# Linear attention's output projection: x seeded into the PSUM banks by identity matmuls and copied back by ScalarE

## The chip, the cores and the metric

The kernel runs on one core of one Trainium2 chip. The metric is the device time of that core in microseconds, from one execution of the whole program; the comparison uses the median of several executions. Five engines of the core appear below: TensorE (PE, with its weight loads listed apart as PEld), VectorE (DVE), ScalarE (ACT), GpSimd (POOL) and SyncE (SP), which only issues transfers here.

## The reference, cut to what matters

The program is a chain of eight residual blocks on `x` of shape (4, 512, 256): four sequences of 512 tokens with 256 channels. Each block adds its result to `x`, or rather to the `x` that the block before it left. The change lies in the fifth block, a gated linear attention with 16 heads; the sixth block, a "workspace" feed-forward, reads the `x` that it leaves.

```python
x = x + _L1_attn_a_ref(_layernorm(x), Wq, Wk, Wv, Wg, Wgk1, Wgk2, bgk2, norm_w, Wo)
x = x + _L1_ffn_ref(_layernorm(x), ...)

def _L1_attn_a_ref(x, ...):            # b = 4, t = 512, h = 16, dk = 8, dv = 16
    q = (x @ Wq).reshape(b, t, h, dk) * scale
    k = (x @ Wk).reshape(b, t, h, dk)
    v = (x @ Wv).reshape(b, t, h, dv)
    gk = jax.nn.log_sigmoid(x @ Wgk1 @ Wgk2 + bgk2) / 16
    def step(S, inp):
        qt, kt, vt, gt = inp
        S = S * jnp.exp(gt)[..., None] + kt[..., None] * vt[..., None, :]
        return S, jnp.einsum('bhk,bhkv->bhv', qt, S)
    _, o = jax.lax.scan(step, S0, (qT, kT, vT, gT))
    g = (x @ Wg).reshape(b, t, h, dv)
    o = o * rsqrt(mean(o * o, -1) + EPS) * norm_w
    o = o * (g * sigmoid(g))
    return o.reshape(b, t, vd) @ Wo     # the projection that the change touches
```

All data are float32.

## The kernel before

**Tiles.** `x[b]` is an SBUF tile of 128 partitions by 4 blocks by 256 channels, one for each sequence, and stays there for the whole program. PSUM has eight banks of 128 x 512 float32. In the linear attention stage they are handed out by three tags: `st` (two buffers of two banks, method `st()`), `two` (one buffer of two banks, method `two()`) and `acc` (two buffers of one bank, method `ps()`). Because `two` has a single buffer, whoever asks for it next waits until the one before has been read out.

**The stage** is `gla_stage` and its inner function `run`. It goes through the four sequences in order, with four steps each (`m` = 0 to 3). The names that the prediction uses:

- `states(b, n, pair)`: TensorE spreads the values into an `st` buffer (L877), VectorE multiplies it by the keys (L878), and two VectorE scans run along the 512 tokens (L881). GpSimd multiplies the scanned states by the queries (L886). Two calls in each step.
- `reads(b, n, qs)`: TensorE sums over the key channels into `acc` banks (L896). It runs one step late. On odd steps ScalarE squares the result (L904) and copies it out (L908), and GpSimd multiplies it by the gate (L910).
- `gate(b)`: at step 0, TensorE projects the gate into `two` (L231, the tile pair `ps_two<-own_xt,s`), and ScalarE applies Silu (L864).
- `output(b, 0)`: TensorE sums the squares over a head (L231, `ps_acc<-gsq,s4b`), VectorE and ScalarE form the reciprocal root (L919 to L926). `output(b, 1)` spreads it with an identity matmul (L231, `ps_acc<-grs,ident`) and VectorE multiplies the result by it (L935; for the last sequence L930 does that directly).
- `output(b, 2)` calls `project_add`, which multiplies by the weights `wo` and adds to `x[b]`. For the first three sequences it uses `two`: eight matmuls of 256 columns (L231, `ps_two<-s,go`), then one VectorE addition over 128 x 1024 (L990). For the last sequence (`halves`) it uses two `acc` banks and two VectorE additions (L988).

**The order of the work.** TensorE's instructions run in the order in which the program writes them (`manual_schedule`). A planner, which simulates the program when it is built, sets the order on the other engines by its own estimates; each engine then runs its list strictly in that order. The program order around the change is this:

```python
if m == 0:
    gate(b)
    if k > 1:
        output(order[k - 2], 2)      # the projection of two sequences ago
...
reads(*held)
output(order[-1], 0)
output(order[-2], 2)                 # the third sequence's projection
self.keep(8, self.st()[:, 0, :])     # eight matmuls with unused results
output(order[-1], 2)                 # the last sequence's, in halves
```

So the first and second sequence's projection stand behind the gate of the third and the fourth sequence; the third's stands in the tail of the stage, ahead of eight filler matmuls (L237) and the last projection.

**What follows `x[b]`.** The next block, method `ws`, takes the layer norm of each `x[b]`: VectorE statistics (L178, L179), a reciprocal root (L141 to L147 on GpSimd for the first two sequences, L154 to L160 otherwise) and ScalarE's normalisation into `ws_xf` (L196), then TensorE transposes (L1096) with copies by ScalarE (L1099) and VectorE (L1100). The planner puts the statistics of the first three sequences into the linear attention stage, directly behind the addition to that `x[b]`.

Of the kernel before, what the change touches and what calls it, by code (L numbers as in the profile page):

```python
# [13 lines left out]
ALU = mybir.AluOpType  # L14
AX = mybir.AxisListType

P = 128
# [4 lines left out]
NC = D // P  # L22
# [3 lines left out]
class Model:  # L26
# [949 lines left out]
    def project_add(self, b, ot, wo, halves=False):  # L976

        if halves:
            pys = [self.ps().rearrange("p (i d) -> p i d", d=D) for _ in range(2)]
        else:  # L980
            py = self.two().rearrange("p a (i d) -> p (a i) d", d=D)
            pys = [py[:, :2], py[:, 2:]]
        for i in range(NI):
            self.mm(pys[i // 2][:, i % 2, :], [(ot[:, c, i * P : (i + 1) * P], wo[:, c, :]) for c in range(NC)])
        x = self.x[b]
        if halves:
            for k, p in enumerate(pys):
                self.nc.vector.tensor_tensor(x[:, 2 * k : 2 * k + 2], x[:, 2 * k : 2 * k + 2], p, op=ALU.add)  # L988
        else:
            self.nc.vector.tensor_tensor(x, x, py, op=ALU.add)  # L990

# [825 lines left out]
```

## Time and profile before

| What | Value |
|---|---|
| Median of 3 runs | 2170.89 us (2170.74 to 2171.37) |
| The profiled execution's own time | 2171.51 us |
| Its span, first to last instruction | 2169.5 us |
| Mean granted TensorE clock | 0.965 of full |
| TensorE matmul busy | 2002.6 us (92%) |
| VectorE busy | 1270.7 us (59%) |
| ScalarE busy | 761.9 us (35%) |
| GpSimd busy | 576.6 us (27%) |

The profile comes from one execution. A row of a group gives the line of the kernel, the engine, the operation, the tile written and the tiles read, the shape and the count; behind the first bar stand the busy time in us and the mean ns of one instruction, behind the second the engine's idle time just before the group and who ended it. A float32 matmul of 128 x 512 appears as two records, so the counts of TensorE are twice the number of matmuls in the program. The chain is the path of work that ended last, in order of time, with start and duration in us.

The state matmuls of the linear attention stage (L877) start between 1401.7 us and 1569.0 us of the span; with the last projections the stage ends shortly before 1600 us. It is about a tenth of the span. VectorE's three additions of L990 start at 1501.8, 1546.3 and 1587.0 us.

### The profile page before, as it was taken

The page shows a single profiled execution, that of the slowest core. Times are in us where ns is not written, and L with a number is a line of the kernel's source. Part 1 is how long each engine was busy: PE and PEld are TensorE (multiplying, and loading weights), DVE is VectorE, ACT ScalarE, POOL GpSimd, SP SyncE. Part 2 cuts the span into 40 slices and gives each one's busy share as a digit, 9 for nine tenths or more (in the row PEclk, how much of TensorE's full clock was granted, in tenths as well). Part 3 has the DMA queues.
Part 4 walks back from the last instruction along what each step waited for, and adds up shares of the span by engine and source line. Part 5 has one row for each costly group of instructions (what it writes and reads, how often), then busy time and mean ns, then how long its engine had stood idle before and what let it go on. Part 6 is the DMA issues. An engine that isn't in the chain of part 4 may idle for free.

```text
span 2169.5 us, 25634 instructions
## 1 busy us (share of the span) xinstructions
PE 2002.6 (92%) x9418; PEld 1069.5 (49%) x9418; DVE 1270.7 (59%) x3180; ACT 761.9 (35%) x1700; POOL 576.6 (27%) x530
## 2 busy tenths in 40 slices
PE   7999999999899999999999999987888889989886
PEld 4556555564544554544454554533345644544464
DVE  5565655756546435644754355498854766666545
ACT  2433444434323222322232233244234334334542
POOL 2333332433312112221312122175620022222100
PEclk9999999999999999999999999989799999999898
DMA  4020000000000000000000000010000000000001
GB/s 176 1 90 1 1 1 1 1 1 1 21 0 0 1 0 0 0 1 0 0 1 0 1 0 1 18 28 0 1 25 1 1 1 1 1 1 2 1 1 40
DMA packets 19838, 22.87 MB, mean 11 GB/s; under 512 B 4833, under 2 KB 17665, under 8 KB 19329
## 3 DMA queue, kind: packets, MB, share of 16 engines
q1 hardware_dynamic: 19712, 21.24, 2.9%
q8 instruction: 74, 1.21, 0.2%
q14 instruction: 52, 0.42, 0.1%
HBM read 19.14 MB, written 2.10 MB: 10 GB/s over the span
## 4 chain that ended last, share of the span: by engine, by line
PE 63%; DVE 16%; issue 11%; ACT 5%; POOL 3%; DMA 1%; SPq 0%; POOLq 0%; DVEq 0%; ACTq 0%
PE ps_two L231 26%; PE ps_acc L231 11%; PE ps_two L383 5%; PE ps_acc L422 3%; PE ps_two L1493 3%; DVE ps_two L249 3%; PE ps_two L410 2%; POOL e L680 2%; PE ps_two L1536 2%; DVE gs L881 1%; PE ps_acc L1241 1%; DVE ln_st L178 1%; PE ps_two L647 1%; ACT prob L390 1%; PE ps_acc L638 1%
## 5 line engine op out<-in xcount | busy, mean ns | idle before, releaser
L680 POOL TENSOR_TENSOR e<-e 128x1024 f32<-128x1024 f32 x64 | 150.6, 2353 | 619.6 <-ACT e L672 592.4
L249 DVE CUSTOM_DVE_ANT_0 ps_two<-ps_two,mask 128x256 f32<-128x256 f32 (+3 forms) x512 | 249.8, 503 | 71.2 <-PE ps_two L383 41.5
L672 ACT ACTIVATE e<-ps_two 128x1024 f32<-128x1024 f32 x128 | 130.6, 1022 | 348.6 <-PE ps_two L231 348.4
L231 PE MATMUL ps_acc<-e,cv 128*128 128x512 f32 x512 | 235.0, 602 | 1.4 <-DVE cot L678 0.9
L231 PE MATMUL ps_two<-cq,ckt 128*128 128x512 f32 x512 | 232.2, 596 | 3.0 <-DVE cq L649 3.0
L395 POOL TENSOR_TENSOR prob<-prob,psum_row 128x256 f32<-128x256 f32 (+3 forms) x128 | 159.5, 1254 | 283.4 <-DVE psum_row L394 277.2
L390 ACT ACTIVATE prob<-ps_two,nmax 128x128 f32<-128x128 f32 (+3 forms) x256 | 132.3, 524 | 147.3 <-DVE nmax L249 138.1
L231 PEld LDWEIGHTS ps_acc<-e,cv 128*128 128x128 f32 x512 | 93.5, 190 | 138.3 <-issue 116.7
L231 PEld LDWEIGHTS ps_two<-cq,ckt 128*128 128x128 f32 x512 | 97.2, 191 | 118.1 <-issue 115.9
L231 PE MATMUL ps_two<-own_xt,s 128*128 128x512 f32 x200 | 110.8, 687 | 18.7 <-DVE prt L129 10.6
L231 PE MATMUL ps_two<-own_xt,s16a 128*128 128x512 f32 x256 | 114.9, 593 | 0.1
L231 PE MATMUL ps_two<-s16b,cot 128*128 128x256 f32 x512 | 113.1, 379 | 0.0
L383 PE MATMUL ps_two<-kvt,qx 64*128 64x256 f32 (+3 forms) x512 | 103.9, 483 | 6.3 <-ACT qx L371 2.4
L1525 ACT ACTIVATE lo_ex<-ps_two 128x1024 f32<-128x1024 f32 (+3 forms) x128 | 85.3, 704 | 69.5 <-PE ps_two L1493 65.9
L410 PEld LDWEIGHTS ps_two<-ident,prob 128*128 128x128 f32 x640 | 71.1, 142 | 73.7 <-issue 48.4
L231 PEld LDWEIGHTS ps_two<-s16b,cot 128*128 128x128 f32 x512 | 97.3, 190 | 20.0 <-issue 7.7
L410 PE MATMUL ps_two<-ident,prob 128*128 128x128 f32 x640 | 94.6, 279 | 12.7 <-ACT qx L371 4.5
L1526 POOL TENSOR_SCALAR_AFFINE_SELECT lo_ex<-lo_ex 128x256 f32<-128x256 f32 x128 | 51.5, 406 | 188.1 <-ACT lo_ex L1525 186.9
L681 DVE TENSOR_TENSOR es<-e 128x512 f32<-128x512 f32 x64 | 43.9, 686 | 94.9 <-POOL e L680 93.8
L383 PE MATMUL ps_two<-kpe,qy 64*128 64x256 f32 (+3 forms) x512 | 90.8, 432 | 0.9 <-POOL qy L317 0.9
L1493 PE MATMUL ps_two<-lo_qm,lo_t 32*128 32x128 f32 (+3 forms) x512 | 75.8, 473 | 11.1 <-ACT lo_ex L1525 4.7
L422 PE MATMUL ps_acc<-prt,kv 128*64 128x256 f32 (+3 forms) x512 | 77.2, 444 | 2.7 <-DVE prt L129 2.7
(428 smaller groups left out, 3423.3 us busy)
## 6 DMA issues: line engine op xcount, KB each, us to landing
x<-in_x SPq DMA_DIRECT2D x4, 512.0 KB, 7.4
s16b<-in_mla_wo SPq DMA_DIRECT2D x1, 2048.0 KB, 18.3
s16a<-in_cos_wq SPq DMA_DIRECT2D x1, 2048.0 KB, 9.9
s16b<-in_cos_wo SPq DMA_DIRECT2D x1, 2048.0 KB, 8.3
out_x<-x SPq DMA_DIRECT2D x4, 512.0 KB, 2.9
s16a<-in_mla_wqn SPq DMA_DIRECT2D x1, 1536.0 KB, 12.2
s<-in_mla_wqa SPq DMA_DIRECT2D x1, 1024.0 KB, 9.2
s4a<-in_mla_wkb SPq DMA_DIRECT2D x1, 512.0 KB, 6.6
```

The source lines that it names most:

```text
L231: self.nc.tensor.matmul(out, lhsT=l, rhs=r, start=k == 0, stop=k == n - 1)
L249: self.nc.vector.tensor_tensor_reduce(out=sc[:, :n], in0=sc[:, :n], in1=self.mask[:, T - n :], scale=-1.0, scalar=3.0e38, op0=ALU.add, op1 ...
L383: nc.tensor.matmul(sc[:, k, :n], lhsT=q[r, rows], rhs=key[r, :n], start=first, stop=not first)
L390: nc.scalar.activation(pr[:, k, :n], sc[:, k, :n], AF.Exp, bias=nm[:, k : k + 1], scale=-1.0, accum_out=sm[:, k : k + 1],)
L395: nc.gpsimd.tensor_tensor(pr[:, :, :n], pr[:, :, :n], sm.unsqueeze(2).to_broadcast([P, 2, n]), op=ALU.mult)
L410: nc.tensor.transpose(pt[:, k, keys], pr[:, k, keys], self.ident)
L422: nc.tensor.matmul(po[k * R : (k + 1) * R, j * P :], lhsT=s.kv[:, j, 0, :], rhs=prt[:, k, j, j * P :], start=j == 0, stop=j == NI - 1,)
L672: nc.scalar.activation(t.e[:, pair * 2 : pair * 2 + 2, :], sc, AF.Exp)
L680: nc.gpsimd.tensor_tensor(e2, t.e[:, 0:2, :], t.e[:, 2:4, :], op=ALU.add)
L1493: nc.tensor.matmul(scs[k // 2][:, k % 2, : keys], lhsT=left[r, rows], rhs=right[r], start=True, stop=True)
L1525: nc.scalar.activation(ex[:, hs, :], sc[:, :, :n], AF.Exp, scale=0.25)
L1526: nc.gpsimd.affine_select(out=ex[:, hs, :P], in_=ex[:, hs, :P], compare_op=ALU.is_ge, fill=0.0, base=0, pattern=[[0, 2], [1, P]], channel_ ...
```

## The change

Only `project_add` is edited, and only the path of the first three sequences (`not halves`) behaves differently. Ahead of the projection, two identity matmuls of 128 x 512 write `x[b]` into the two banks of the projection's buffer, with `start=True`; the eight projection matmuls then accumulate onto that with `start=False`. VectorE's addition to `x[b]` goes, and a ScalarE copy from the banks to `x[b]` takes its place. The last sequence's path is written out by hand, with the same flags as before.

```diff
             py = self.two().rearrange("p a (i d) -> p (a i) d", d=D)
             pys = [py[:, :2], py[:, 2:]]
+        x = self.x[b]
+        if not halves:
+            for k in range(2):
+                self.nc.tensor.matmul(
+                    pys[k].rearrange("p i d -> p (i d)"), lhsT=self.ident,
+                    rhs=x[:, 2 * k : 2 * k + 2].rearrange("p i d -> p (i d)"), start=True, stop=False,
+                )
         for i in range(NI):
-            self.mm(pys[i // 2][:, i % 2, :], [(ot[:, c, i * P : (i + 1) * P], wo[:, c, :]) for c in range(NC)])
-        x = self.x[b]
+            for c in range(NC):
+                self.nc.tensor.matmul(
+                    pys[i // 2][:, i % 2, :], lhsT=ot[:, c, i * P : (i + 1) * P], rhs=wo[:, c, :],
+                    start=halves and c == 0, stop=c == NC - 1 and (halves or i % 2 == 1),
+                )
         if halves:
             for k, p in enumerate(pys):
                 self.nc.vector.tensor_tensor(x[:, 2 * k : 2 * k + 2], x[:, 2 * k : 2 * k + 2], p, op=ALU.add)
         else:
-            self.nc.vector.tensor_tensor(x, x, py, op=ALU.add)
+            self.nc.scalar.copy(x, py)
```

The matmuls of the projection no longer go through the helper `mm`, so in a profile of the changed kernel they stand on a line of `project_add` and not on L231.

## The prediction

> **What bounds the kernel now.** I read the page first, then the chain of waits through the stage, then the timeline of single engines around each of the three additions, and last the granted clock in short stretches. The page says that TensorE is the busiest engine:
>
> ```profile
> PE 2002.6 (92%) x9418; PEld 1069.5 (49%) x9418; DVE 1270.7 (59%) x3180; ACT 761.9 (35%) x1700; POOL 576.6 (27%) x530
> ```
>
> That is an average. In the linear attention stage the stretch from 1409 to 1578 us has VectorE busy for 144.7 of 169 us and TensorE for 141.5, so they share the limit there, and what counts is who waits for whom at the edited lines. The groups of instructions in that part, for VectorE:
>
> ```profile
> L990 DVE TENSOR_TENSOR x<-x,ps_two 128x1024 f32<-128x1024 f32 x2 | 2.4, 1221 | 10.2 <-PE ps_two L231 10.2
> ```
>
> The two additions cost 2.4 us, but VectorE stood idle for 10.2 us ahead of them, waiting for the projection. TensorE sets the pace there. The chain of waits shows the same at the first addition, in order of time (start, duration):
>
> ```profile
> 1496.95 1.03 ACT gg L864
> 1497.98 0.04 issue
> 1498.03 3.73 PE ps_two L231 x16
> 1501.76 0.02 issue
> 1501.78 1.23 DVE x L990
> 1503.02 0.02 issue
> 1503.04 1.40 DVE ln_st L178 x4
> 1504.44 0.21 DVE ln_mv L179 x3
> 1504.66 1.12 DVE ps_st L878
> ```
>
> The reader is to see an unbroken path: the gate's Silu frees the single `two` buffer, the projection runs at once, the addition follows, then the statistics of that `x[b]`, then the next state multiplication. At 1541.43 to 1549.14 the chain repeats these pieces for the second sequence. In the tail it runs over TensorE:
>
> ```profile
> 1577.28 1.49 PE ps_acc L896 x4
> 1578.77 3.12 PE ps_acc L231 x4
> 1581.89 3.45 PE ps_two L231 x16
> 1585.35 6.87 PE ps_st L237 x16
> 1592.21 3.47 PE ps_acc L231 x16
> 1595.68 0.02 issue
> 1595.70 0.69 DVE x L988
> ```
>
> Here TensorE works without a gap from the head sums through the third projection, the eight fillers and the last projection; the third addition (L990 at 1586.97) is off the path.
>
> **The change part by part.**
>
> *Added on TensorE: two identity matmuls of 128 x 512 for each of three sequences.* The nearest rows are the head sums, which are two float32 matmuls of the same shape. The timeline of TensorE:
>
> ```profile
> 1505.55 1.88 PE L231 MATMUL ps_acc<-gsq,s4b 128*128 128x512 f32 x4
> 1507.36 1.13 PE L877 MATMUL ps_st<-gv,s4b 32*128 32x512 f32 x4
> ```
>
> Two matmuls are four records; their weight loads start 0.43 us apart, so the pair takes 4 x 0.43 = 1.72 us (1.81 from start to the next instruction's start). At half clock it would be 3.4 us, but the granted clock is 1.00 from 1498 to 1504, from 1542 to 1550 and from 1582 to 1592, where the new matmuls land. They can't use TensorE's 1.11 us of idle time ahead of the projection: they write the same `two` buffer, which Silu has to free first. So all 1.72 us lie on the path, three times. The weights and x are there long before: no new wait and no DMA.
>
> *Removed from VectorE, added on ScalarE.* The addition took 1.22 us. The copy is like `gv<-ps_two` (L848, 128 x 1024 from the same banks), 1.00 to 1.01 us. It sits on the path as the addition did, since the statistics need x. Here a rule speaks against the change: the Trainium skill, page "ScalarE: Activation LUTs", section "Rules for kernel authors", gives simple arithmetic to VectorE because it is up to about three times as fast per element in bf16. The data here are float32 in PSUM, and the rows say 1.01 against 1.22: 0.21 us saved each time. By the rule a 1.22 us addition would become a copy of up to 3.7 us, and the two first sequences would lose 2.5 us each more. I take the rows.
>
> *What is queued behind the moved wait.* On ScalarE the copy now waits for the projection; behind it stand the square and copy of the read-out (L904, L908), which wait for matmuls that TensorE runs after the projection (1.0 us, about as long as the copy) and so lose nothing but the 1.72 us. ScalarE was idle for 3.56 us there. On GpSimd the gating multiplication (L910) waits for L908, with 3.99 us idle before it. The `two` buffer is freed 1.5 us later, and its next user (L1031, 1508.42) comes 4.9 us after the old release. All these are covered; without the cover the copy's 1.0 us would be added. SP and POOL issue nothing new.
>
> *First and second sequence.* If the planner keeps the statistics ahead of the state multiplication, VectorE resumes later by 1.72 - 0.21 = 1.51 us. If it puts the state multiplication first, that waits only for its own matmuls: old end 1502.67 + 1.13 = 1503.80, new 1505.52, against an old start of 1504.58: 0.97 us later, with the statistics in VectorE's idle 2.6 us at 1516. I take the first, which is the order of now: 2 x 1.51 = 3.0 us. Does anything absorb it? From 1504.6 the chain goes over scans, GpSimd (L886, L840), ScalarE (L842, L1036) and TensorE to the next gate without slack, so nothing does.
>
> *Third sequence.* The chain is TensorE's own: 1.72 us later. VectorE is relieved of 1.22 us in that tail, but its input for the last projection (L930, ready at 1591.29) already beats the end of the fillers, so relief gains nothing. From L988 on everything moves.
>
> Sum: 3.0 + 1.7 = 4.7 us. Against the profiled execution (2171.51 us, span 2169.5) that gives 2176.2; that execution lies 0.6 us above the median of the runs, so against the median: 2170.89 + 4.7 = 2175.6 us.
>
> *The clock, unknown in both directions.* Granted clock by stretch (us, busy, clock):
>
> ```profile
> 1510.00:1514.00 4.00, 1.86 (x13) 1.00 0.00 0
> 1530.00:1533.00 3.00, 0.71 (x4) 1.00 0.00 0
> 1535.00:1537.00 2.00, 2.00 (x4) 0.50 0.00 0
> 1558.00:1560.00 2.00, 2.00 (x16) 0.50 0.00 0
> ```
>
> A pause of 2.14 us at 1511.6 left the clock alone; pauses of 2.58 us at 1530.7 and 2.54 us at 1554.4 halved it, the former for about 6.6 us of gate matmuls. The Trainium skill, page "TensorE: Matmul & The Clock Gate", Part 1, tells of a free-running window of 3.4 us, and its rule is that only gaps longer than a window hurt. By that rule none of these pauses would have halved the clock and a shift of 1.5 us would change nothing; by the rows shorter ones do, and the placing of a pause against the windows can decide. So a shift can cost one window at half clock at 1515 (1.7 us), or win up to half of the 6.6 us at 1534 (3.3 us). I set zero and keep -3.3 and +1.7 as ends.
>
> **The rivals.**
>
> *VectorE is the bound, and TensorE hides the new work.* For it: 86% busy, and L990 is on the chain twice. Then three additions leave, 3 x 1.22 = 3.7 us: 2167.2 us, not slower. It decides where VectorE would reach L990 after the projection's end; in the profile it reaches it 4.26 and 5.91 us before. Against it: those idle times, more than twice the added 1.72 us.
>
> *The clock pays it back.* The second gate at full clock gives 3.3 us back, and the milder order of the planner (0.97 in place of 1.51) another 1.1: 4.7 - 4.4 = 0.3, about 2171.2 us. For it: pauses near the deciding length. Against it: nothing makes the shift land well.
>
> *The planner places the copy badly.* Its order of ScalarE is new. If the copy goes behind L904 and L908, it starts when these end, about 1.0 + 1.1 us after the projection, and VectorE's statistics wait in front of the state multiplication: 1.51 + 2.1 = 3.6 us for each of two sequences, 9.0 with the tail, 2179.9 us. Against it: the copy is ready first. A reshuffle elsewhere belongs here too, in both directions.
>
> The change not doing what it says: an identity matmul of float32 could only be cheaper than the rows if it were not float32, and the program gives no other type.
>
> **How the numbers follow.** The serial case (+4.7, with its own range of 3.5 to 6.5 from planner order and clock) has 0.57; the clock paying back (-1 to +3.5) 0.15; bad placing (+6.5 to +10) 0.15; VectorE bound, or a new order of the planner that happens to be lucky (-2 and below), 0.13. 0.2% of the time is 4.3 us, about what a measurement of this kernel can tell from no change; 4.7 is hardly beyond it. Of the serial case some 0.42 lies above the bound and 0.15 below; with bad placing, slower is 0.57. The last case lies beyond the bound with 0.1, where only a lucky order reaches, and inside it with 0.03, where the 3.7 us of a bound VectorE lie: faster is 0.1, within is 0.15 + 0.15 + 0.03 = 0.33. The range leaves out that last case, 0.13, below 2169.5 us, and of bad placing 0.07 above 2180.5 us.
>
> **What would show it.** In the profile after: four records of `ps_two<-ident,x` per sequence, some 1.7 us, directly behind Silu; L990 gone; a copy of 1.0 us on ScalarE; TensorE busy up by about 5 us, VectorE down by 3.7; VectorE's idle time ahead of its next work up from 4.3 and 5.9 us by about 2.7 (1.72 + 1.0); the fillers ending 4.7 us later against the span. It is wrong if the gap between the second gate's end and the next state multiplication does not grow, if the tail does not move by 1.7 us, or if rows outside this stage change their length.

## The result and the profile after

| What | Before | Changed |
|---|---|---|
| Median of 14 executions each | 2171.93 us (2168.85 to 2178.52) | 2181.04 us (2171.82 to 2186.19) |
| Ratio, changed to before | | 1.0036 [1.0027, 1.0045] |
| Ratio in a second measurement (22 and 61 executions) | | 1.0028 [1.0018, 1.0037] |
| The profiled execution: its own time, span | 2171.51 us, 2169.5 us | 2171.82 us, 2170.0 us |
| Mean granted clock of the profiled execution | 0.965 | 0.971 |

The change makes the kernel slower by 6.1 us (second measurement) to 7.8 us (first), which is a ratio minus one, times 2171 us. (The plain difference of the two medians is 9.1 us; single executions spread over 14 us, and the three figures agree no better than that allows.) The forecast was +4.7 us: the right sign, and smaller than either figure, though the interval of the second measurement, +3.9 to +8.0 us, still holds it.

One warning comes first. The two profiled executions have nearly the same time, and the profile of the changed kernel is the shortest of its 14 executions. The time of an execution goes with its mean granted clock: at 0.965 the changed kernel took 2183.8 us (mean of 4), at 0.967 2179.6 us (mean of 3), and the profiled one had 0.971. So the loss can't be read from the two spans; it has to be read stretch by stretch, between instructions that both kernels have.

That the loss as a whole is not just a lower clock can be seen from executions of equal mean clock. In the second measurement, at 0.966 the changed kernel took 2182.0 us (mean of 5) and the kernel before 2174.6 (7), at 0.968 2179.4 (3) and 2173.2 (18), at 0.971 2176.4 (3) and 2169.8 (3): 6 to 7 us more each time.

The first line of the page shows the work that was added and removed:

```profile
PE 1995.7 (92%) x9430; PEld 1065.3 (49%) x9430; DVE 1265.8 (58%) x3177; ACT 765.8 (35%) x1703; POOL 577.2 (27%) x530
```

Twelve more matmul records, three instructions fewer on VectorE and three more on ScalarE: the program is what the diff says. TensorE's busy time is nevertheless 6.9 us lower than before; a matmul's record gets longer at a lower clock, and this execution had the higher one.

The groups between 1490 and 1600 us (ScalarE's between 1409 and 1600), with busy time and mean ns of one, then the idle time before:

```profile
L992 PE MATMUL ps_two<-s,go 128*128 128x256 f32 x48 | 10.8, 379 | 0.0
L986 PE MATMUL ps_two<-x,ident 128*128 128x512 f32 x12 | 5.8, 610 | 2.2 <-ACT gg L864 2.2
L1000 ACT COPY x<-ps_two 128x1024 f32<-128x1024 f32 x3 | 3.0, 1012 | 11.5 <-PE ps_two L992 11.5
```

The chain of waits through the first addition, in order of time (start, duration), answers to the one shown of before:

```profile
1495.08 1.98 PE ps_two L986 x4
1497.06 3.47 PE ps_two L992 x16
1500.53 0.02 issue
1500.55 1.02 ACT x L1000
1501.57 0.02 issue
1501.60 1.41 DVE ln_st L178 x4
1503.00 0.28 DVE ln_mv L179 x4
1503.28 1.13 DVE ps_st L878
```

The identity matmuls (L986) stand in the path between Silu and the projection, and the copy (L1000) stands where VectorE's addition stood. In the tail the path is TensorE's own, with the identity matmuls in it:

```profile
1577.82 1.52 PE ps_acc L896 x4
1579.34 3.10 PE ps_acc L231 x4
1582.43 1.72 PE ps_two L986 x4
1584.15 3.45 PE ps_two L992 x16
1587.61 6.87 PE ps_st L237 x16
1594.47 3.47 PE ps_acc L992 x16
1597.94 0.02 issue
1597.96 0.69 DVE x L998
```

To compare the kernels I measure the time between the same instructions in each trace: the start of the first state matmul of the linear attention, the end of the last addition to `x[3]`, the MAX8 of each workspace block, and the start of ScalarE's last copy of `lo_og` in the block between (the LoRA attention; L1541 before, L1551 in the changed kernel). "Again" is a second profile of the changed kernel.

| Stretch (us) | Before | Changed | Again |
|---|---|---|---|
| start of the span to the first state matmul | 1401.68 | 1398.68 | 1399.19 |
| linear attention, to the last addition to `x[3]` | 194.71 | 199.97 | 199.93 |
| to the first MAX8 of the first workspace block | 13.59 | 13.75 | 13.70 |
| to the last `lo_og` copy of the LoRA attention | 425.97 | 421.52 | 421.54 |
| to the first MAX8 of the second workspace block | 20.80 | 23.22 | 23.23 |
| to the second MAX8 of that block | 59.63 | 59.71 | 59.67 |

Two rows carry the loss: the edited stage, +5.26 us, and a block 450 us later that no line of the diff touches, +2.42 us. Together they are 7.7 us. The rows that give back (the unedited blocks ahead of the stage, and those up to the end of the LoRA attention) are where the profiled executions had different clocks. Three stretches between two of ScalarE's copies in the LoRA attention, of before and then of the changed kernel, with TensorE's busy time and the granted clock:

```profile
1774.37:1795.83 21.46, 19.58 (x132) 0.92 0.01 2
1893.09:1907.30 14.21, 12.66 (x108) 0.88 0.00 1
2016.98:2028.51 11.53, 9.87 (x100) 1.00 0.01 1
```

```profile
1774.14:1793.78 19.64, 17.95 (x132) 1.00 0.01 2
1891.56:1904.16 12.60, 11.05 (x108) 1.00 0.00 1
2013.32:2026.49 13.17, 11.51 (x100) 0.87 0.01 1
```

The counts are the same in each pair. Wherever the clock is lower, the stretch is 1.6 to 1.8 us longer, in one kernel or the other.

### The second workspace block

VectorE's instructions there in the changed kernel (start, total duration of the row, engine, line, tiles; in brackets idle time before and who ended it):

```profile
2049.88 0.69 DVE L1110 COPY ws_xt<-ps_two 128x512 f32<-128x512 f32 x1 [2.29 <-ACT ws_xt L1109]
2050.49 0.17 DVE L157 TENSOR_TENSOR ws_rp<-ws_rp,ws_ms 128x16 f32<-128x16 f32 x1
2051.72 0.69 DVE L1110 COPY ws_xt<-ps_two 128x512 f32<-128x512 f32 x1 [1.07 <-ACT ws_xt L1109]
2052.33 0.16 DVE L158 SCALAR_TENSOR_TENSOR ws_rp<-ws_rp,ws_ms 128x16 f32<-128x16 f32 x1
2052.53 0.69 DVE L163 SCALAR_TENSOR_TENSOR ws_norm<-ws_rp,ws_ms 128x512 f32<-128x512 f32 x1
```

and in the kernel before:

```profile
2051.62 0.17 DVE L157 TENSOR_TENSOR ws_rp<-ws_rp,ws_ms 128x16 f32<-128x16 f32 x1 [2.01 <-ACT ws_ms L156]
2051.83 0.17 DVE L158 SCALAR_TENSOR_TENSOR ws_rp<-ws_rp,ws_ms 128x16 f32<-128x16 f32 x1
2052.04 0.69 DVE L163 SCALAR_TENSOR_TENSOR ws_norm<-ws_rp,ws_ms 128x512 f32<-128x512 f32 x1
2052.65 0.68 DVE L1100 COPY ws_xt<-ps_two 128x512 f32<-128x512 f32 x1
2053.74 0.69 DVE L1100 COPY ws_xt<-ps_two 128x512 f32<-128x512 f32 x1 [0.41 <-ACT ws_xt L1099]
```

These are the same five instructions in another order. Before, the norm's three instructions (L157, L158, L163) run first and the two copies of `ws_xt` follow. In the changed kernel both copies stand ahead of the norm's last two, and they wait for 2.29 and 1.07 us. L163 starts 16.1 us after the start of ScalarE's last `lo_og` copy before (2052.04 - 2035.95) and 18.6 us after it in the changed kernel (2052.53 - 2033.92), and TensorE's transposes of the norm wait for it:

```profile
2050.03 1.04 PE L1106 MATMUL ps_two<-ident,ws_xf 128*128 128x128 f32 x8
2053.27 1.16 PE L1118 MATMUL ps_acc<-ident,ws_norm 128*128 128x128 f32 x8 [2.21 <-DVE ws_norm L163]
```

Before, TensorE had no such wait:

```profile
2052.93 1.06 PE L1108 MATMUL ps_acc<-ident,ws_norm 128*128 128x128 f32 x8
```

The mean granted clock over this stretch is 0.92 before and 0.93 in the changed kernel, so the clock does not make the difference. The planner simulates the whole program and deals out VectorE's list by estimated times, so a shift of its estimates in the linear attention can come out as another order here; two kernels below, e9 and e10, test that.

### The profile page after: what moved, and what is told of

Read it like the earlier page. It is cut to its first block, busy times and chain, and to the rows that moved or that the text cites. A ratio compares the mean times of both kernels' runs of the same rounds, so it can differ in the third digit from the quotient of the medians.

```text
span 2170.0 us, 25657 instructions
## 1 busy us (share of the span) xinstructions
PE 1995.7 (92%) x9430; PEld 1065.3 (49%) x9430; DVE 1265.8 (58%) x3177; ACT 765.8 (35%) x1703; POOL 577.2 (27%) x530
## 4 chain that ended last, share of the span: by engine, by line
PE 63%; DVE 17%; issue 11%; ACT 5%; POOL 3%; DMA 1%; SPq 0%; POOLq 0%; DVEq 0%; ACTq 0%
PE ps_two L231 26%; PE ps_acc L231 10%; PE ps_two L383 5%; PE ps_acc L422 3%; PE ps_two L1503 3%; DVE ps_two L249 3%; PE ps_two L410 2%; POOL e L680 2%; PE ps_two L1546 2%; DVE gs L881 2%; DVE ln_st L178 1%; PE ps_acc L1251 1%; PE ps_two L647 1%; ACT prob L390 1%; DVE ps_st L878 1%
## 5 line engine op out<-in xcount | busy, mean ns | idle before, releaser
L231 PE MATMUL ps_acc<-e,cv 128*128 128x512 f32 x512 | 235.0, 602 | 1.4 <-DVE cot L678 0.9
L231 PE MATMUL ps_two<-cq,ckt 128*128 128x512 f32 x512 | 232.2, 596 | 3.0 <-DVE cq L649 3.0
L231 PEld LDWEIGHTS ps_acc<-e,cv 128*128 128x128 f32 x512 | 93.5, 190 | 138.4 <-issue 116.7
L231 PEld LDWEIGHTS ps_two<-cq,ckt 128*128 128x128 f32 x512 | 97.2, 191 | 118.0 <-issue 115.6
L231 PE MATMUL ps_two<-own_xt,s 128*128 128x512 f32 x200 | 111.6, 691 | 18.6 <-DVE prt L129 10.6
L231 PE MATMUL ps_two<-own_xt,s16a 128*128 128x512 f32 x256 | 114.9, 592 | 0.1
L231 PE MATMUL ps_two<-s16b,cot 128*128 128x256 f32 x512 | 113.1, 379 | 0.0
L231 PEld LDWEIGHTS ps_two<-s16b,cot 128*128 128x128 f32 x512 | 97.3, 190 | 20.1 <-issue 7.7
```

What stands on the lines that cost most here:

```text
L231: self.nc.tensor.matmul(out, lhsT=l, rhs=r, start=k == 0, stop=k == n - 1)
```

## The experiments

Each kernel was timed against the kernel before in five rounds, and one execution of each was profiled. The stretches are those of the table above.

### Parts of the change

**e1_identities_alone.** The identity matmuls stay, but the projection overwrites them, and VectorE adds as before.

```diff
-  rhs=x[:, 2 * k : 2 * k + 2]..., start=True, stop=False,
+  rhs=x[:, 2 * k : 2 * k + 2]..., start=True, stop=True,
-  start=halves and c == 0, stop=c == NC - 1 and (halves or i % 2 == 1),
+  start=c == 0, stop=c == NC - 1,
-            self.nc.scalar.copy(x, py)
+            self.nc.vector.tensor_tensor(x, x, py, op=ALU.add)
```

> The six identity matmuls are issued as in the change, but the projection overwrites them (start on its own first matmul), and VectorE's addition stays. Theory S (the added TensorE time is serial, and nothing else matters): 3 x 1.72 = 5.2 us slower than before, ratio about 1.0024. Theory O (the planner's new order in the stages after, which this kernel shares with the changed one, costs about 3 us on top): 8 us, ratio 1.0037. Theory V (VectorE's relief was worth something, so without it things get worse than in the changed kernel): 9 us or more.

Measured: 2179.72 us against 2172.31, ratio 1.0023 [1.0013, 1.0034]. The stage is 200.23 us, +5.5: TensorE's added work alone brings as much as the whole change does there (+5.26). The second workspace block's first stretch is 23.23 us here too. So the traces have what theory O describes, while the timed loss, +5.0 us, is that of theory S; this gap comes back in the last table.

**e2_copy_alone.** No identity matmuls; ScalarE copies the bare projection to `x[b]`, so the residual of the first three sequences is left out of the result.

```diff
-            self.nc.vector.tensor_tensor(x, x, py, op=ALU.add)
+            self.nc.scalar.copy(x, py)
```

> No identity matmuls; ScalarE copies the projection to x, so the residual of the first three sequences is left out. The planner's order after the stage is that of before. Theory S: two times 0.21 us for the shorter copy and nothing in the tail: 0.4 us faster, not to be told from no change. Theory V (VectorE is the bound): up to 3.7 us faster, ratio 0.9983. If the copy on ScalarE delays its neighbours: slower by 1 to 2 us.

Measured: 2172.29 us against 2172.31, ratio 0.9999 [0.9989, 1.0009]; stage 194.20 us, -0.5. VectorE is three additions lighter, 3.7 us, and almost nothing of it arrives; the 0.5 us are about the two copies that are 0.21 us shorter each. After the copy VectorE had been waiting:

```profile
1503.47 1.40 DVE L178 BATCH_NORM_STATS2 ln_st<-x 128x6 f32<-128x256 f32 x4 [3.61 <-ACT x L990]
```

The addition was no work in VectorE's way, it was the first thing VectorE did after a wait. The rival that VectorE is the bound falls with this run.

**e3_third_alone** and **e4_first_two.** The change for some of the sequences only.

```diff
-        if not halves:
+        seeded = b in (2,)          # e4: (0, 1)
+        if seeded:
...
-        else:
+        elif seeded:
             self.nc.scalar.copy(x, py)
+        else:
+            self.nc.vector.tensor_tensor(x, x, py, op=ALU.add)
```

> Identity matmuls and ScalarE copy for the third sequence alone; the first two as before. Theory S: TensorE's tail is 1.72 us longer, ratio 1.0008. If VectorE's relief in the tail counted: 0 or below. In the profile the eight fillers end 1.7 us later behind the third projection's start, and VectorE is ready for the last projection 4 us before TensorE gets to it.

> Identity matmuls and ScalarE copy for the first and second sequence; the third as before. Theory S: 2 x 1.51 = 3.0 us slower, ratio 1.0014. Theory O: its order in the later stages is nearly that of the changed kernel, so about 3 us more, 6 us or 1.0028. If the clock decides, somewhere between 0 and 5 us, with the gate's matmuls of other lengths in the profile.

Measured: e3 2180.04 us, 1.0022 [1.0011, 1.0033]; e4 2180.58 us, 1.0033 [1.0021, 1.0044]. In the traces the stage grew by 1.75 us in e3 and 4.39 us in e4. e3's stage is the forecast for the third sequence (1.72). e4 also has the new order in the second workspace block (23.22 us), so its 4.4 + 2.4 - 0.5 (in the first workspace block) = 6.3 us agree with its time (ratio 1.0033, +7.2 [4.6, 9.6]). Its stage grew by more than the 3.0 us expected partly because of the tail, which e4 leaves with VectorE's addition. There the last projection had to wait for VectorE, one of whose instructions (L925) took 2.69 us where it took 0.61 before; why, no run shows:

```profile
1596.15 3.69 PE L993 MATMUL ps_acc<-s,go 128*128 128x256 f32 x16 [0.71 <-DVE go L930]
```

e3 has the old order there (20.78 us), and its time, +4.8 [2.4, 7.2], is more than its stage accounts for. Its lists differ from those of before in the LoRA attention as well, where ScalarE's copy of `lo_v` comes ahead of exponentials, and one of TensorE's matmuls waits for it (a row of the timeline of TensorE in e3):

```profile
1865.43 0.49 PE L1506 MATMUL ps_two<-lo_qm,lo_t 32*128 32x128 f32 x4 [1.27 <-ACT lo_v L1472]
```

Before, the same matmul waited 0.54 us, for another instruction; that is 0.7 us, of which the projection behind it gives 0.54 back, as it waited for VectorE before and does not in e3. Another matmul of that block (L1506 at 1857.16) waits 1.33 us for `lo_wvob` where it did not wait before. The whole stretch of the LoRA attention is 2.9 us longer in e3's profile and the part behind the second block's first MAX8 2.1 us shorter; how much of either is order and how much clock is not settled, and so neither are e3's other 3 us. The two parts don't add up to the whole (the timed losses sum to more than the change's own), so a part run alone brings a new order of its own and can't be read as a share of the change.

### The changed kernel again, with fewer fillers

**e5_after_again** is the changed kernel; **e6_after_keep7** and **e7_after_keep3** have fewer fillers; **e8_third_keep3** is e3's kernel with three.

```diff
-            self.keep(8, self.st()[:, 0, :])
+            self.keep(7, self.st()[:, 0, :])     # e7, e8: 3
```

> The changed kernel once more, with a second profile and more runs. Theory S+O (the stage costs 5.3 us in the two profiles, and the planner's new order in the second workspace block another 2.4 us): 7 to 8 us slower than before, ratio about 1.0035; in the profile the stage is again 5 us longer than before's 194.7 us, and the stretch from the last read-out copy of the fourth sequence's attention to the second block's first maximum is 23.2 us against 20.8. Theory K (the clock alone makes the extra over 4.7 us): the stretch is not always 23.2 us, or the stage is within 1 us of before's.

> The changed kernel with seven fillers in place of eight in the tail. One filler is 0.86 us. In this build the planner happens to put VectorE's norm ahead of the last two copies in the second workspace block, as before. Theory O: that stretch is 20.8 us and not 23.2, so with the filler the kernel is 3.3 us faster than the changed one, about 4 us slower than before, ratio 1.002. If the order is without effect: the stretch stays at 23.2 us or the time moves by 0.9 us alone.

> The changed kernel with three fillers in place of eight. In the changed kernel's profile the last projection's input was ready at 1589.7 us and TensorE got to it at 1594.3, 4.6 us later, so five fillers (4.3 us) can go. Theory S: the stage is 200.0 - 4.3 = 195.7 us, 1 us over before; this build has the old order in the second workspace block, so the total is about 1 us over before too, ratio 1.0005. If the fillers keep the clock up: the last projection runs at half clock and 3 us come back.

> The version that the traces point to: identity matmuls and copy for the third sequence alone, where VectorE's relief is worth something once the fillers make room for it: three fillers, the first two sequences as before. Theory S: 194.7 + 1.72 - 4.3 = 192.1 us for the stage, 2.6 us faster than before, ratio 0.9988. If the last projection's input becomes the bound, it starts at 1589.7 in place of 1592.0 us: 2.3 us. If the clock drops: no gain.

| Kernel | Time (us) | Ratio | Stage | First block's MAX8 | Second block's MAX8 |
|---|---|---|---|---|---|
| before | 2173.27 | | 194.71 | 13.59 | 20.80 |
| e5_after_again | 2179.56 | 1.0028 [1.0018, 1.0037] | 199.93 | 13.70 | 23.23 |
| e6_after_keep7 | 2177.73 | 1.0022 [1.0013, 1.0031] | 202.14 | 14.01 | 21.58 |
| e7_after_keep3 | 2176.12 | 1.0011 [1.0003, 1.0019] | 196.08 | 14.71 | 20.80 |
| e8_third_keep3 | 2172.95 | 0.9999 [0.9989, 1.0009] | 193.75 | 14.82 | 20.81 |

e5 repeats the result and, to within 0.05 us, the stretches that lose. e6's stage is no measure of a filler: its profiled execution lost 3.1 us against the changed kernel's ahead of the edited line, with a granted clock of 0.70 from 1429 to 1436 us and a third gate (L231, eight records) of 5.95 us; its timed loss is 1.3 us smaller than the changed kernel's by the ratios, which agrees with one filler (0.86 us) and an order that costs 0.8 us instead of 2.4, within the intervals. The order was not the one expected: VectorE's list has one of the last two copies ahead of the norm and one behind it, and the stretch, 21.58 us, lies between the other two values.

e7 takes out five fillers, 5 x 0.86 = 4.3 us. Its stage is 3.9 us shorter and the old order is back (20.80 us). It still isn't faster than before: the next block takes 1.1 us more. The start of that block in e7, on TensorE and on ScalarE:

```profile
1599.60 0.77 PE L1106 MATMUL ps_two<-ident,ws_xf 128*128 128x128 f32 x5 [0.16 <-ACT ws_xf L196]
1602.85 2.08 PE L237 MATMUL ps_two<-mask,ident 128*128 128x512 f32 x2 [2.49 <-DVE ws_xt L1110]
```

```profile
1595.52 5.99 ACT L196 ACTIVATE ws_xf<-x,ln_off,ln_rstd 128x256 f32<-128x256 f32 x12
```

ScalarE's twelve normalisations of the first three sequences stand in its list behind the reciprocal root of the third sequence (L155, L156), which waits for VectorE's statistics of that sequence. In e7 they start at 1595.52 us, and TensorE comes to the transposes of the first sequences at 1596.93, only 1.4 us later; in the changed kernel with eight fillers it comes 5.9 us later (1591.90 and 1597.76). So in e7 the transposes can go no faster than one normalisation after the other, 0.49 us each. They wait three times, and the 16 end 3.44 us after their start, where with eight fillers the same 16 took 1.91 us without a wait. e8 shows the same: its stage is 0.96 us shorter than before, its next block 1.23 us longer, and the timed sum is nothing. In e8's profile the stage also holds a piece at half clock ahead of the edited line (1491.9 to 1498.7 us, 6.8 us where the kernel before has 3.4) that cost 1.6 us; without it the stage would be 2.5 us shorter, which is about the 2.6 that were expected, and half of that goes to the next block. None of these kernels beat the kernel before.

### The order in the second workspace block

Up to here the new order and the longer stretch only went together. Two more kernels separate the order from the change.

**e9_before_keep9** is the kernel before with nine fillers, and **e10_after_keep4** is the changed kernel with four.

```diff
-            self.keep(8, self.st()[:, 0, :])
+            self.keep(9, self.st()[:, 0, :])     # e9, in the kernel before
```

```diff
-            self.keep(8, self.st()[:, 0, :])
+            self.keep(4, self.st()[:, 0, :])     # e10, in the changed kernel
```

> The kernel before with nine filler matmuls in the tail where it has eight; the linear attention code is not touched otherwise. Its built lists show VectorE in the second workspace block with both copies of ws_xt ahead of the norm, as the changed kernel has it, and not the order of the kernel before. Theory (2.4 us of the loss come from that new order, which any edit can bring about): the stage gets longer by one filler, 6.87 / 8 = +0.86 us, and the stretch up to the MAX8 of the second workspace block is 23.2 us instead of 20.8, with TensorE waiting about 2.2 us for ws_norm; together +3.3 us, a ratio near 1.0015. Rival (that stretch got longer through something that the identity matmuls or the ScalarE copy leave behind, such as the clock): the stretch stays at 20.8 us, and the time is +0.9 us.

> The changed kernel with four filler matmuls where it has eight. One filler more than the run with three, and its built lists show the changed kernel's VectorE order in the second workspace block (both ws_xt copies ahead of the norm), where the run with three had the order of the kernel before. Theory of the order: the stage is 4 x 0.86 = 3.4 us shorter than in the changed kernel (196.5 us against 199.9), the stretch up to the second block's MAX8 is 23.2 us as in the changed kernel, against 20.8 with three fillers; so it is some 2.8 us above the run with three fillers, a ratio near 1.0025. Rival (the fillers themselves, through the clock after them, set that stretch): it stays near 20.8 us, as with three fillers, and the ratio near 1.001 to 1.0015.

Measured, e9: stage 195.63 us (+0.92), second block's MAX8 after 23.23 us. No identity matmul, no copy, and the stretch is as long as in the changed kernel. The wait in e9's trace is the same one:

```profile
2050.18 1.04 PE L1096 MATMUL ps_two<-ident,ws_xf 128*128 128x128 f32 x8
2053.43 1.16 PE L1108 MATMUL ps_acc<-ident,ws_norm 128*128 128x128 f32 x8 [2.21 <-DVE ws_norm L163]
```

e10: stage 195.99 us and 23.23 us, where e7 with one filler less has 20.80:

```profile
2050.36 1.16 PE L1118 MATMUL ps_acc<-ident,ws_norm 128*128 128x128 f32 x8 [2.21 <-DVE ws_norm L163]
```

So the stretch follows the order of VectorE's list and nothing else that was varied: 23.2 us with both copies ahead of the norm (the changed kernel twice, e1, e4, e9, e10), 21.6 us with one (e6) and 20.8 us with the norm ahead of the last two (before, e2, e3, e7, e8). The clock is no rival: each of these stretches has a mean granted clock of 0.92 or 0.93. The times are too coarse for 2.4 us in a single pair: e9 has 1.0007 [0.9997, 1.0016], which holds the expected 1.0015 and also the rival's 0.9 us, and e10 has 1.0011 [1.0000, 1.0021], the same ratio as e7, so the timing does not show the 2.8 us by which it was expected to lie above e7. The order is shown by the traces, not by these times.

## Why the prediction was right, and what it left out

**The step per sequence was right.** From the start of the identity matmuls or the projection to the start of the next state multiplication (L878) the first sequence takes 8.12 us where it took 6.55: +1.57 us, forecast +1.51. The second has the same, 8.12 for 6.55, again +1.57. The copy measured 1.01 us against the addition's 1.22, as its neighbour `gv<-ps_two` had told. The rule that gives simple arithmetic to VectorE (Trainium skill, "ScalarE: Activation LUTs", "Rules for kernel authors") takes its factor of three from bf16 and operations with a single source, and this addition is float32 with two sources; read as if it held here, it would have made a loss of an estimated 2.5 us per sequence, and the measured 0.21 us gained decides against that reading. VectorE kept its statistics ahead of the state multiplication, and ScalarE ran the copy ahead of the square of the read-out:

```profile
1500.55 1.01 ACT L1000 COPY x<-ps_two 128x1024 f32<-128x1024 f32 x1 [4.23 <-PE ps_two L992]
1501.60 0.60 ACT L904 ACTIVATE gsq<-ps_acc 128x512 f32<-128x512 f32 x1
```

The rival of a badly placed copy did not happen. Two readings on the way were slightly off without effect: by its own figures the milder order would be 0.94 us later (1505.52 against 1504.58), not 0.97, and the next user of `two` came 5.4 us after the old release (1508.42 against 1503.00), not 4.9.

**The tail was right.** From the head sums on, all of TensorE's rows stand 1.7 us later and follow without a gap; the piece grew by 1.69 us, forecast 1.72. VectorE's relief there was worth nothing, as e2 shows.

**The clock was right as a pair of ends, and its zero was luck.** That the placing of a pause decides, and not its length alone, is what the traces show (the last section). The forecast named a window at half clock at 1515 us as the loss and the gate at 1534 us as the gain. The loss came. It fell on the projection of the fourth sequence's values, which has a gate's tile names but is read out as `gv` (L848), before and then in the changed kernel:

```profile
1513.75 3.70 PE L231 MATMUL ps_two<-own_xt,s 128*128 128x512 f32 x8 [2.14 <-ACT ws_kq L1036]
```

```profile
1512.37 5.40 PE L231 MATMUL ps_two<-own_xt,s 128*128 128x512 f32 x8 [2.00 <-ACT ws_kq L1046]
```

In the changed kernel the granted clock was 0.50 from 1513.42 to 1516.83 us (the rows are in the last section), where before it was 1.00 throughout. That is about +1.6 us from the start of the pause to the end of that projection, after a pause that was shorter than before. The gain came elsewhere than at the gate named: the gate at 1535 us still has 0.50, but the small matmuls that follow, at half clock from 1558 us before, ran at 1.00 there:

```profile
1558.00:1560.00 2.00, 1.19 (x7) 1.00 0.00 0
```

From the state matmuls behind the pause (L877, at 1556.91 before and 1558.81 in the changed kernel) to the state multiplication that waits for the matmuls after them (L878, at 1566.10 and 1566.64) it is 7.83 us where it was 9.19, -1.36. Together +0.3: the forecast had no reason to expect that the two nearly cancel.

**The sum of the stage** is then 1.57 + 1.57 + 1.69 + 0.3 = 5.1 us, against 5.26 measured and 4.7 forecast.

**What failed is the step that set everything outside the stage to nothing.** The text said "From L988 on everything moves", that is, by the same amount, and put a reshuffle of the planner elsewhere in a rival's last sentence, without a price, "in both directions". It cost +2.4 us, half as much again as the sum. Its own test would have found it: "if rows outside this stage change their length". The total of 7.7 us therefore lies in the bracket of the last rival (+6.5 to +10) though the mechanism that gave that bracket its size (a copy behind the read-out) didn't act. The range held by the ratio (1.0036 x 2170.89 = 2178.7 us, under its top of 2180.5); the median of 2181.04 itself is half a microsecond above it, beside a kernel before that measured 1.0 us higher than in the three executions the forecast started from.

How far three stretches (stage, first block's MAX8, second block's MAX8) account for the time of each kernel, against before; the timed loss is the ratio minus one, times 2172 us, and uncertain by about 2 us each:

| Kernel | Three stretches (us) | Timed loss (us) |
|---|---|---|
| changed, again | +7.8, +7.8 | +7.8, +6.1 |
| e1 identities alone | +8.7 | +5.0 |
| e2 copy alone | -0.5 | -0.2 |
| e3 third alone | +2.1 | +4.8 |
| e4 first two | +6.3 | +7.2 |
| e6 (7 fillers) | +8.6 | +4.8 |
| e7 (3 fillers) | +2.5 | +2.4 |
| e8 (third alone, 3 fillers) | +0.3 | -0.2 |
| e9 (before, 9 fillers) | +2.9 | +1.5 |
| e10 (4 fillers) | +3.7 | +2.4 |

Most agree. The stretches come from one execution each, clock included, and the three leave out what e3 and e8 have in other places. e6 is the one whose profiled execution had a low clock within the stage; e1 and e3 are off by 3.7 and 2.7 us in opposite directions, and what lies behind that stays open.

## What to carry to other kernels

An addition that also brings the result out of PSUM, right after a wait, is hardly saved by moving it into the matmul accumulation: a copy has to bring the result out in its place (here 1.01 us for 1.22), and the seeding matmuls are serial work on the engine that the others wait for (1.72 us). So ask first who was idle ahead of the instruction that is to go. Where a planner deals out the engines' lists from a simulation of the whole program, every edit is also an edit of distant stages: compare the order of each engine's instructions and the times between common landmarks before explaining a difference, and price a reshuffle in the forecast. Where the clock moves single executions by more than the effect, one profile shows where time went but not how much was lost in total.

## What the runs showed of the hardware

A pause of 2.14 us left TensorE's clock at 1.00 and one of 2.00 us at nearly the same place was followed by a stretch at 0.50, so the pause's length alone did not decide. The traces show more than that. Every stretch at half clock that begins and ends within the span, in all twelve traces, lasts 3.41 us or two to five times that, and within an execution all of them begin and end on one grid with a step of 3.41 us. Cut at the edges of that grid, the two pauses look like this, before and then in the changed kernel (TensorE's busy time, count, clock):

```profile
1509.49:1512.91 3.42, 2.12 (x14) 1.00 0.00 0
1512.91:1516.32 3.41, 2.57 (x6) 1.00 0.00 0
```

```profile
1510.01:1513.42 3.41, 1.41 (x5) 1.00 0.00 0
1513.42:1516.83 3.41, 3.41 (x6) 0.50 0.00 0
1516.83:1520.25 3.42, 3.13 (x15) 1.00 0.00 0
```

Before, an edge of the grid cuts the pause in two, and no window is less than 62% busy; in the changed kernel the pause lies within one window, which is 41% busy, and the next one is at half clock. Counted over the twelve traces, of the windows at full clock in which TensorE was busy for less than 40%, 133 of 133 were followed by one at half clock; at 40 to 70% it was 175 of 551, and at 70% or more 2 of 6404. So the busy share of a window goes with the clock of the next one, and between 40 and 70% something else, which these traces don't show, takes part.

The Trainium skill ("TensorE: Matmul & The Clock Gate", Part 1) has the free-running window of 3.4 us too, but gives as its abstract rule to avoid idle gaps longer than that; beside it, it tells of a kernel whose frequent short idles between groups of matmuls made the clock swing. In these traces single pauses of 2.0 to 2.6 us were enough where they fell within one window, and the measurement decides.

Which pauses were hit changed from kernel to kernel, at about 1.6 us for each stretch of one window. The time of an execution goes along with its mean clock, closely in the changed kernel (0.965 to 0.971 in the first measurement, from 2186.2 to 2171.8 us) and more loosely in the kernel before, where executions at 0.967 took 2169.5 to 2178.0 us.
